# Masks of shifted attention windows as TensorE products, and layer 3's last addition on ScalarE, in a four-layer image kernel

## Chip, core and metric

The kernel runs on one core of one Trainium2 chip. The time is device microseconds from launch to end; the smaller the better. The median of the runs shown is 4648.1 us. All data are 32-bit floats.

The core has five engines that run side by side and wait for one another by semaphores: TensorE (PE: products, with its weight loads listed apart as PEld), VectorE (DVE), ScalarE (ACT), GpSimd (POOL), and SyncE (SP), whose queue issues the DMAs here. Products land in PSUM, of which the kernel uses six single banks and one pair of banks.

## What is computed

32 images of 56 x 56 pixels and 96 channels go through four layers. Cut to what matters here:

```python
# layer 0: mixture of 4 experts by a router; 96 -> 384 channels, 3x3 depthwise, 384 -> 96
rw = sigmoid(mean(x) @ Wr + br)
h = relu(bn(x @ (rw-mixed Wpw) + ...)); h = relu(bn(depthwise3x3(h, rw-mixed Wdw) + ...))
x = x + bn(h @ (rw-mixed Wpwl) + ...)
# layer 1: x + depthwise 5x5; layer 2: relu, depthwise 3x3, 96 -> 96 product, batch norm
# layer 3: one block of shifted-window attention
shifted = roll(x, (-3, -3)); win = 7x7 windows (64 of them, 49 pixels each)
h = layernorm(win); q, k, v = h @ wq, h @ wk, h @ wv          # 3 heads of 32
attn = softmax(q k^T / sqrt(32) + mask)     # mask: -inf between pixels of different groups
res = x + unroll((attn v) @ wo + bo)
x = res + gelu(layernorm(res) @ w1 + b1) @ w2 + b2
```

The mask matters only in windows of the last column (their pixels with column >= 4 come from the other side of the image) and of the last row (row >= 4 likewise); the corner window has four groups.

## The kernel before

Four stages run as a software pipeline over the images: the router of one image, the conditional layer 0 of the image before it, the depthwise layers 1 and 2 of the one before that, and layer 3 (called swin) of the oldest. Each stage is a Python generator that records its work; `interleave` gives each piece of work a target from `PLAN` (start and length of each stage, in images). The class `Recorder` then lays out one fixed order for each engine: it runs through a model of the engines with the costs of `COST`, takes at each moment the ready work with the lowest target, and uses `CROSSING` for the time from one engine's end to another's start and `TO_TENSOR` for that to TensorE. Nothing is decided on the chip: each engine works through its list, waiting by semaphore. As every recorded instruction is issued by `give`, all of them have one line in the profile, L578, and are told apart by tile names.

Two kinds of filler are written into the orders. If the model's TensorE has nothing to do for `SPARE_AFTER` ns, a spare product is put in (identity by identity, 128 x 128, rows banks<-ident). Between two long taps on VectorE other work, or else a one-element fill (breath), is put in. Both are then executed whether or not the chip needs them. A 32-bit product shows as two matmul records and two weight loads.

What works where, by names of tiles:

- Layer 0: matmuls banks<-xT,wmix (96 to 384 channels), ScalarE into h; nine taps of the depthwise filter on h, one on ScalarE and eight on VectorE (h<-h,mix,h, 1568 elements, 48 an image); matmuls banks<-h,wmix, added to xT by VectorE. All of xT is rearranged by DMA for layers 1 and 2.
- Layers 1 and 2: matmuls banks<-x,band in 32 x 32 sub-arrays, four banks at a time; ScalarE moves the outputs; DMAs into filtered; matmul banks<-pw,filtered into res. The weights pw have a 97th column, so that res carries, beside 96 values centred on their mean, the mean itself.
- Layer 3 by rows of windows, i = 0 to 7: `norm1` and `turn1` (ScalarE squares lnsq, VectorE sum var, GpSimd power and product lnd, TensorE transposes banks<-ident,lnd); products with wq, wk, wv; `exponentials`: scores banks<-qT,kT, 24 products (8 windows by 3 heads) in one group of sub-arrays of 32 rows by 64 columns, three banks, then ScalarE's exp into exps; `kept`: GpSimd multiplies exps by a mask of zeros and ones, in rows 0 to 6 only the last window (exps<-exps,keep_column), in row 7 all (keep_last); `averaged`: sums of exponentials (pair<-exps,ones) and weighted values (pair<-exps,v) into the one pair of banks, ScalarE's log and exp for the reciprocal; `divided`: three VectorE operations that end in oT and free the pair; `attended`: product with wo, added to res.
- The end of layer 3 in chunks of 4 and 3 tiles of 112 pixels, `hidden` and `perceptron`: products with w1, ScalarE's gelu into hid, products with w2 (banks<-w,hid). GpSimd writes tb = res + b2; VectorE then adds, for each of the 4 or 3 tiles, the bank, the mean (the 97th column of res) and tb; SyncE sends tb out. There are two tb buffers.

The constants of the order, and the lines at the end of layer 3 that the change touches:

```python
CROSSING = 136
TO_TENSOR = {"vector": 981, "gpsimd": 1497, "scalar": 453, "sync": 1437}
SPARE_AFTER = 318
...
tbs = ring("tb", [LT, 4, C], 2)
...
chip.gpsimd.tensor_tensor(tb, src[:, :, :C], b2[:LT, None, :].to_broadcast([LT, n, C]), ALU.add)
...
for j in range(n):
    chip.vector.scalar_tensor_tensor(
        tb[:, j], pt[:LT, j * C : (j + 1) * C], src[:, j, C:], tb[:, j], ALU.add, ALU.add
    )
```

Of the kernel before, what the change touches and what calls it, by code (L numbers as in the profile page):

```python
# [13 lines left out]
AF = mybir.ActivationFunctionType  # L14
ALU = mybir.AluOpType
# [4 lines left out]
C = 96  # L20
# [3 lines left out]
P = 128  # L24
NB = 3
NROW = 8
RT = 7 * W
PK = 98
NP = 4
LT = 2 * W  # L30
NL = 7
PW = 14
WT = 49
NWIN = 8
SLOT = 64
PS = SLOT + WT
# [9 lines left out]
NH = 3  # L46
HD = C // NH
# [3 lines left out]
NEG = -1e30  # L51
# [22 lines left out]
    return m  # L74


def window_keeps():


    r, c = np.divmod(np.arange(WT), 7)  # L80
    last = np.zeros((P, NP, WT), np.float32)
    column = np.zeros((P, WT), np.float32)
    for j in range(NP):
        for at in range(2):
            group = np.where(r >= 4, 2, 0) + np.where((c >= 4) & (j == NP - 1) & (at == 1), 1, 0)
            last[SLOT * at : SLOT * at + WT, j] = group[:, None] == group[None, :]
    column[SLOT : SLOT + WT] = (c[:, None] >= 4) == (c[None, :] >= 4)
    return last, column


def banded(k, back):
# [67 lines left out]
LANDING = 2200  # L159
IMAGE_LANDING = 10000  # L160

PLAN = {"router": (-0.309, 1.019), "conditional": (0.642, 1.103), "depthwise": (1.462, 1.483), "swin": (3.316, 0.933)}
CROSSING = 136

TO_TENSOR = {"vector": 981, "gpsimd": 1497, "scalar": 453, "sync": 1437}
SPARE_AFTER = 318
RUN = 1
CHANGE = 170
SAME = 0.0
BESIDE = {(32, 32): 16, (32, 64): 6, (64, 32): 6, (32, P): 3, (P, 32): 3, (P, P): 1}  # L170


# [409 lines left out]
def kernel(  # L582
# [10 lines left out]
    def ring(name, shape, n):  # L593
        return Ring([const.tile(shape, F32, name=f"{name}{k}") for k in range(n)])
# [15 lines left out]
    qTs = ring("qT", [C, RT], 2)  # L610
    kTs = ring("kT", [C, RT if general else NWIN * SLOT], 2)
    vs = ring("v", [P, NP, C], 3)
    tbs = ring("tb", [LT, 4, C], 2)
    x3s = ring("x3", [P, NQ, NBLK, W + 3], 2)
    oTs = ring("oT", [C + 1, 2 * RT], 2)
    x1s = ring("x1", [P, NQ, NBLK, W + 4], 2)
# [48 lines left out]
    for at, name in (  # L665
# [4 lines left out]
        src = a[name]  # L670
        if len(src.shape) == 1:
            src = src.rearrange("(o m) -> o m", o=1)
        elif len(src.shape) == 4:
            src = src.rearrange("e a b m -> (e a b) m")
        nc.sync.dma_start(out=rows[at : at + src.shape[0]], in_=src)
    c384 = const.tile([P, NB, NV], F32, name="c384")
    for k in range(NB):
        pt = mm.tiles[k]
# [4 lines left out]
    for at, name in (  # L683
# [4 lines left out]
        src = a[name]  # L688
        if len(src.shape) == 1:
            src = src.rearrange("(o m) -> o m", o=1)  # L690
        elif len(src.shape) == 4:
            src = src.rearrange("a b o m -> (a b o) m")
        nc.sync.dma_start(out=rows96[at : at + src.shape[0]], in_=src)
    c96 = const.tile([C, NU], F32, name="c96")
    pt = mm.tiles[3]
# [31 lines left out]
    pt = mm.tiles[5]  # L727
# [11 lines left out]
    def later(shape, src, name):  # L739
        return hold(const.tile(shape, F32, name=name), src)  # L740
# [14 lines left out]
    pt = mm.tiles[4]  # L755
# [15 lines left out]
    b2 = later([P, C], a["L3_conv_b2"].partition_broadcast(P), "L3_conv_b2")  # L771
    if general:
        masks = later([PK, 2, NP * PK], layouts["mask"].rearrange("l q j k -> q l (j k)"), "masks")
    else:
        keep_last = later([P, NP, WT], layouts["keep_last"], "keep_last")
        keep_column = later([P, WT], layouts["keep_column"], "keep_column")

        slots = ring("slots", [C, NWIN, SLOT], 3)

        exps = ring("exps", [P, NH, NP, WT], 2)  # L780
        ones32 = const.tile([P, HD], F32, name="ones32")
# [61 lines left out]
    chip = Recorder(nc)  # L843
# [326 lines left out]
    def stage_swin(b, res):  # L1170
# [52 lines left out]
        def exponentials(i):  # L1223

            qT, kT = rows_of[i][:2]
            pss = [chip.new(mm) for _ in range(NH)]
            with chip.together():
                for j in range(NP):
                    for at in range(2):
                        n = 2 * j + at  # L1230
                        for h in range(NH):
                            hs = slice(h * HD, (h + 1) * HD)
                            chip.tensor.matmul(
                                pss[h][SLOT * at : SLOT * (at + 1), j * WT : (j + 1) * WT],
                                kT[hs, SLOT * n : SLOT * (n + 1)],
                                qT[hs, WT * n : WT * (n + 1)],
                                start=True,
                                stop=True,
                            )
            e = exps_of[i] = chip.new(exps)  # L1240
            for h in range(NH):
                chip.scalar.activation(
                    e[:, h].rearrange("k j q -> k (j q)").part(h),
                    pss[h][:, : NP * WT],
                    AF.Exp,
                    scale=1.0 / math.sqrt(HD),
                    reads=(tables,),
                )

        every = tuple(range(NH))  # L1250

        def kept(i):
            e = exps_of[i].part(*every)
            if i < NROW - 1:
                ks = slice(SLOT, PS)
                view = e[ks, :, NP - 1]
                chip.gpsimd.tensor_tensor(
                    view, view, keep_column[ks, None, :].to_broadcast([WT, NH, WT]), ALU.mult
                )
                return  # L1260
            keep = keep_last.rearrange("k j q -> k (j q)")
            view = e.rearrange("k h j q -> k h (j q)")
            chip.gpsimd.tensor_tensor(view, view, keep[:, None, :].to_broadcast([P, NH, NP * WT]), ALU.mult)

        def averaged(i):

# [138 lines left out]
        def perceptron(i):  # L1405
            src, n = chunk(res, i)
            tb = chip.new(tbs)[:, :n]
            chip.gpsimd.tensor_tensor(tb, src[:, :, :C], b2[:LT, None, :].to_broadcast([LT, n, C]), ALU.add)
            active = [hiddens.pop((i, k)) for k in range(NB)]
            pt = chip.new(mm)  # L1410
            with chip.together():
                for j in range(n):
                    for k in range(NB):
                        chip.tensor.matmul(
                            pt[:LT, j * C : (j + 1) * C],
                            active[k][:, j * LT : (j + 1) * LT],
                            w2[:, k],
                            start=(k == 0),
                            stop=(k == NB - 1),
                        )  # L1420
            for j in range(n):
                chip.vector.scalar_tensor_tensor(
                    tb[:, j], pt[:LT, j * C : (j + 1) * C], src[:, j, C:], tb[:, j], ALU.add, ALU.add
                )
            to = out[b, i // 2].rearrange("(j p) c -> p j c", p=LT)
            chip.sync.dma_start(out=to[:, 4:] if i % 2 else to[:, :4], in_=tb)

# [2 lines left out]
        exps_of, turned_out = {}, {}  # L1430
# [58 lines left out]
        for i in range(NROW + 1) if general else ():  # L1489
            before, here, after = i > 0, i < NROW, i + 1 < NROW  # L1490
# [40 lines left out]
        for i in range(NROW + 2) if not general else ():  # L1531
            here, after = i < NROW, i + 1 < NROW
            if here:
                exponentials(i)
                yield 1.5
            if after:
                project_q(i + 1)
                yield 2
            if here:
                kept(i)  # L1540
            if i + 3 < NROW:
                norm1(i + 3)
                yield 1
            if after:
                project_v(i + 1)
                yield 1
            if 0 < i <= NROW:
                averaged(i - 1)
                yield 1.5
                divided(i - 1)  # L1550
                yield 1
            if i > 1:
                attended(i - 2)
                yield 1.5
            if i >= NROW - 1:
                norm2(i - NROW + 1)
                yield 1
            turn1(i + 2)
            yield 0.5
# [36 lines left out]
    def when(stage, b):  # L1596

        start, length = PLAN[stage]
        return b + start, length
# [23 lines left out]
def build(nc, shapes, batch):  # L1623

    a = {k: nc.dram_tensor(f"in_{k}", s, F32, kind="ExternalInput").ap() for k, s in shapes.items()}
    layouts = {
        k: nc.dram_tensor(f"in_{k}", s, F32, kind="ExternalInput").ap()
        for k, s in (
            ("mask", (2, PK, NP, PK)), ("keep_last", (P, NP, WT)), ("keep_column", (P, WT)),
            ("k5", (P, NSLOT, 5, 2 * BIN)), ("k3", (P, NSLOT, 3, 2 * BIN)), ("centre", (P, 2 * BIN)),  # L1630
        )
    }

    out = nc.dram_tensor("out", (batch, NROW // 2, 2 * RT, C), F32, kind="ExternalOutput").ap()
    with tile.TileContext(nc) as tc, tc.tile_pool(name="flags", bufs=1) as flags:
        in_range = flags.tile([1, 1], mybir.dt.int32, name="in_range")
        tile_scores_in_range(tc, a, in_range)
        kernel(tc, a, layouts, out, False)

        with tc.If(nc.values_load(in_range[:1, :1]) < 1):  # L1640
            kernel(tc, a, layouts, out, True)
# [23 lines left out]
```

## Time and profile before

| | |
|---|---|
| runs shown | 4643.1, 4648.1, 4649.3 us; median 4648.1 |
| profiled execution, its own time | 4639.0 us |
| its span, first to last instruction | 4637.2 us |
| mean granted TensorE clock | 0.992 |
| scores on TensorE (banks<-qT,kT) | 12288 records, 198.5 us busy |
| spare products (banks<-ident) | 1246 records, 170.7 us busy |
| masks on GpSimd | 224 of 1769 ns and 32 of 1508 ns on average |
| tb on GpSimd (res + b2) | 256, 1994 ns on average |
| tb on VectorE (bank + mean + tb) | 896, 308 ns on average |
| taps on VectorE | 1536, 1890 ns on average |

The span holds a start of some 0.3 ms in which the pipeline fills, a long steady part that repeats for each image, and an end in which only layers 1 to 3 are left. A share of busy time over the whole span mixes these. Where a row gives a count and a mean, their product can be more than the busy time, since matmuls of different sub-arrays overlap. In a row of waits the three numbers are the sum in us, how often, and the longest. In the busy time by window, each engine's us is followed by its instructions; the granted clock, the DMA share and GB/s come last. In the timeline, an item is start, duration, engine, line, operation, tiles, shape and count, and in brackets the idle time before it with what ended it.

### The profile page before, as it was taken

The page shows a single profiled execution, that of the slowest core. Times are in us where ns is not written, and L with a number is a line of the kernel's source. Part 1 is how long each engine was busy: PE and PEld are TensorE (multiplying, and loading weights), DVE is VectorE, ACT ScalarE, POOL GpSimd, SP SyncE. Part 2 cuts the span into 40 slices and gives each one's busy share as a digit, 9 for nine tenths or more (in the row PEclk, how much of TensorE's full clock was granted, in tenths as well). Part 3 has the DMA queues.
Part 4 walks back from the last instruction along what each step waited for, and adds up shares of the span by engine and source line. Part 5 has one row for each costly group of instructions (what it writes and reads, how often), then busy time and mean ns, then how long its engine had stood idle before and what let it go on. Part 6 is the DMA issues. An engine that isn't in the chain of part 4 may idle for free. (4 is left out here: it accounts for less than half of the span.)

```text
span 4637.2 us, 166483 instructions
## 1 busy us (share of the span) xinstructions
PE 4489.9 (97%) x71978; PEld 3168.6 (68%) x71978; DVE 4061.4 (88%) x5444; ACT 3393.6 (73%) x6625; POOL 2967.1 (64%) x1855
## 2 busy tenths in 40 slices
PE   5799999999999999999999999999999999999999
PEld 3566767676767676666676766666766676766677
DVE  6999999998999998999998999988999999999733
ACT  2467777777777777777787777777777787777666
POOL 3035767666767766767766767766767666767633
PEclk8999999999999999999999999999999999999999
DMA  2112111122111122211121211121211122211110
GB/s 54 34 39 45 41 43 32 39 48 45 44 41 30 38 47 45 45 40 30 38 47 45 46 40 30 38 45 45 46 41 30 38 45 45 46 41 31 28 36 22
DMA packets 556411, 185.36 MB, mean 40 GB/s; under 512 B 551679, under 2 KB 552340, under 8 KB 552596
## 3 DMA queue, kind: packets, MB, share of 16 engines
q1 hardware_dynamic: 555668, 174.61, 16.9%
q8 instruction: 569, 9.32, 0.9%
q14 instruction: 174, 1.43, 0.1%
HBM read 42.37 MB, written 38.54 MB: 17 GB/s over the span
## 5 line engine op out<-in xcount | busy, mean ns | idle before, releaser
L578 DVE SCALAR_TENSOR_TENSOR h<-h,mix,h 128x1568 f32<-128x1568 f32 x1536 | 2892.2, 1890 | 18.7 <-ACT h L578 13.0
L578 POOL TENSOR_TENSOR var<-var,mhalf 112x4 f32<-112x4 f32 (+1 forms) x512 | 1068.8, 2093 | 195.4 <-DVE var L578 182.8
L578 POOL TENSOR_TENSOR lnd<-res,var 112x384 f32<-112x384 f32 (+1 forms) x512 | 779.1, 1528 | 524.7 <-PE banks L578 503.0
L578 ACT ACTIVATE hid<-banks,c 128x448 f32<-128x448 f32 (+1 forms) x768 | 446.4, 589 | 346.5 <-PE banks L578 340.4
L578 PE MATMUL banks<-xT,wmix 96*128 96x392 f32 (+1 forms) x1536 | 644.2, 519 | 5.7 <-DVE wmix L578 4.5
L578 PE MATMUL banks<-hT,w 96*128 96x448 f32 (+1 forms) x1536 | 641.0, 507 | 3.7
L578 PE MATMUL banks<-x,band 32*32 32x280 f32 x24576 | 611.7, 408 | 14.8 <-issue 7.7
L578 PEld LDWEIGHTS banks<-w,hid 128*112 128x112 f32 x5376 | 563.9, 178 | 75.9 <-issue 46.2
L578 POOL TENSOR_TENSOR tb<-res,L_conv_b 112x384 f32<-112x384 f32 (+1 forms) x256 | 506.3, 1994 | 160.0 <-DMA out<-tb 139.1
L578 PE MATMUL banks<-w,hid 128*112 128x96 f32 x5376 | 576.2, 262 | 5.1 <-ACT hid L578 4.6
L578 PE MATMUL banks<-h,wmix 128*96 128x392 f32 x1536 | 548.4, 497 | 11.6 <-ACT h L578 11.6
L578 ACT ACTIVATE h<-banks,bias,s 128x392 f32<-128x392 f32 (+1 forms) x768 | 518.3, 690 | 39.0 <-PE banks L578 29.6
L578 PEld LDWEIGHTS banks<-x,band 32*32 32x32 f32 x24576 | 385.0, 103 | 226.7 <-issue 50.7
L578 POOL TENSOR_TENSOR exps<-exps,keep_column 49x147 f32<-49x147 f32 x224 | 396.2, 1769 | 204.1 <-ACT exps L578 194.0
L578 ACT ACTIVATE h<-h,biasd,s 128x784 f32<-128x784 f32 x384 | 389.3, 1038 | 114.0 <-DVE breath L578 83.6
L578 PEld LDWEIGHTS banks<-h,wmix 128*96 128x96 f32 x1536 | 246.5, 164 | 248.6 <-issue 207.2
L578 PEld LDWEIGHTS banks<-xT,wmix 96*128 96x128 f32 x1536 | 266.0, 192 | 134.0 <-issue 57.6
L578 DVE TENSOR_REDUCE var<-lnsq 112x4 f32<-112x388 f32 (+1 forms) x512 | 253.7, 496 | 113.3 <-ACT lnsq L578 59.8
L578 ACT ACTIVATE h<-h,mix 128x1568 f32<-128x1568 f32 x192 | 308.6, 1607 | 60.4 <-PE banks L578 46.4
L578 DVE SCALAR_TENSOR_TENSOR tb<-banks,res,tb 112x96 f32<-112x96 f32 x896 | 246.6, 308 | 109.2 <-PE banks L578 103.9
L578 PEld LDWEIGHTS banks<-hT,w 96*128 96x128 f32 x1536 | 252.5, 191 | 128.9 <-issue 69.1
L578 PEld LDWEIGHTS banks<-ident,lnd 112*96 112x96 f32 x1792 | 197.5, 126 | 157.0 <-issue 127.3
(135 smaller groups left out, 6653.0 us busy)
## 6 DMA issues: line engine op xcount, KB each, us to landing
x<-xT SPq DMA_DIRECT2D x1536, 35.0 KB
xT<-in_x SPq DMA_DIRECT2D x32, 1176.0 KB
filtered<-x SPq DMA_DIRECT2D x960, 35.0 KB
out<-tb SPq DMA_DIRECT2D x128, 168.0 KB
out<-tb SPq DMA_DIRECT2D x128, 126.0 KB
filtered<-x SPq DMA_DIRECT2D x576, 7.0 KB
band<-in_k SPq DMA_DIRECT2D x1, 960.0 KB
wpw<-in_L_conv_Wpw SPq DMA_DIRECT2D x1, 576.0 KB
```

The costliest lines, as they stand in the source:

```text
L578: getattr(getattr(self.nc, w.engine), method)(*args, **kw)
```

## The change

The masks are no longer applied after the exponential but added to the scores before it. For each window that has groups, each head gets one more product, 4 group indicators of the keys by 4 rows of 0 or -1e30 of the queries (in sub-arrays of 32 rows and 64 columns like the scores; unused rows are zero), which accumulates on the score. In rows 0 to 6 that is the last window (3 products), in row 7 all eight (24). GpSimd's products by masks (`kept`) go.

At the end of layer 3, ScalarE writes tb = res + mean, one activation for each tile of 112 pixels; GpSimd adds b2 to tb in place; VectorE adds the bank to all of tb in one instruction. There are three tb buffers in place of two.

The constants of the order (`PLAN`, `CROSSING`, `TO_TENSOR`, `SPARE_AFTER`) have other values, so that the lists of all engines are laid out anew. The title of the change also names layer 0's product in whole columns; no line of layer 0 differs.

```diff
-PLAN = {"router": (-0.309, 1.019), "conditional": (0.642, 1.103), "depthwise": (1.462, 1.483), "swin": (3.316, 0.933)}
-CROSSING = 136
-TO_TENSOR = {"vector": 981, "gpsimd": 1497, "scalar": 453, "sync": 1437}
-SPARE_AFTER = 318
+PLAN = {"router": (-0.16, 0.924), "conditional": (0.642, 1.103), "depthwise": (1.452, 1.424), "swin": (3.369, 1.066)}
+CROSSING = 412
+TO_TENSOR = {"vector": 926, "gpsimd": 798, "scalar": 129, "sync": 1437}
+SPARE_AFTER = 431
...
-def window_keeps():
+def window_groups():
...
+    keys = np.zeros((C, 4, SLOT), np.float32)
+    queries = np.zeros((C, 4, WT), np.float32)
+    for kind in range(4):
+        group = np.where(c >= 4, 1, 0) * (kind % 2) + np.where(r >= 4, 2, 0) * (kind // 2)
+        for h in range(NH):
+            for g in range(4):
+                keys[h * HD + g, kind, :WT] = group == g
+                queries[h * HD + g, kind] = np.where(group == g, 0.0, NEG)
+    return keys, queries
...
-    tbs = ring("tb", [LT, 4, C], 2)
+    tbs = ring("tb", [LT, 4, C], 3)
...
-        keep_last = later([P, NP, WT], layouts["keep_last"], "keep_last")
-        keep_column = later([P, WT], layouts["keep_column"], "keep_column")
+        group_keys = later([C, 4, SLOT], layouts["group_keys"], "group_keys")
+        group_queries = later([C, 4, WT], layouts["group_queries"], "group_queries")
...
                         n = 2 * j + at
+                        kind = int(n == NWIN - 1) + 2 * int(i == NROW - 1)
                         for h in range(NH):
...
+                            into = pss[h][SLOT * at : SLOT * (at + 1), j * WT : (j + 1) * WT]
                             chip.tensor.matmul(
-                                pss[h][SLOT * at : SLOT * (at + 1), j * WT : (j + 1) * WT],
+                                into,
                                 kT[hs, SLOT * n : SLOT * (n + 1)],
                                 qT[hs, WT * n : WT * (n + 1)],
                                 start=True,
-                                stop=True,
+                                stop=not kind,
+                            )
+                        for h in range(NH if kind else 0):
+                            hs = slice(h * HD, (h + 1) * HD)
+                            into = pss[h][SLOT * at : SLOT * (at + 1), j * WT : (j + 1) * WT]
+                            chip.tensor.matmul(
+                                into, group_keys[hs, kind], group_queries[hs, kind], start=False, stop=True
                             )
...
-        def kept(i):
-            e = exps_of[i].part(*every)
-            if i < NROW - 1:
-                ks = slice(SLOT, PS)
-                view = e[ks, :, NP - 1]
-                chip.gpsimd.tensor_tensor(
-                    view, view, keep_column[ks, None, :].to_broadcast([WT, NH, WT]), ALU.mult
-                )
-                return
-            keep = keep_last.rearrange("k j q -> k (j q)")
-            view = e.rearrange("k h j q -> k h (j q)")
-            chip.gpsimd.tensor_tensor(view, view, keep[:, None, :].to_broadcast([P, NH, NP * WT]), ALU.mult)
...
             tb = chip.new(tbs)[:, :n]
-            chip.gpsimd.tensor_tensor(tb, src[:, :, :C], b2[:LT, None, :].to_broadcast([LT, n, C]), ALU.add)
+            for j in range(n):
+                chip.scalar.activation(tb[:, j], src[:, j, :C], AF.Identity, bias=src[:, j, C:])
+            chip.gpsimd.tensor_tensor(tb, tb, b2[:LT, None, :].to_broadcast([LT, n, C]), ALU.add)
...
-            for j in range(n):
-                chip.vector.scalar_tensor_tensor(
-                    tb[:, j], pt[:LT, j * C : (j + 1) * C], src[:, j, C:], tb[:, j], ALU.add, ALU.add
-                )
+            chip.vector.tensor_tensor(
+                tb, pt[:LT, : n * C].rearrange("p (j c) -> p j c", c=C), tb, ALU.add
+            )
...
-            if here:
-                kept(i)
```

## The prediction

> **What bounds the kernel now.** I read the page's busy shares first, then one steady stretch of the busy times by window, the list of waits, and last the timeline of TensorE.
>
> ```profile
> span 4637.2 us, 166483 instructions
> PE 4489.9 (97%) x71978; PEld 3168.6 (68%) x71978; DVE 4061.4 (88%) x5444; ACT 3393.6 (73%) x6625; POOL 2967.1 (64%) x1855
> ...
> 2000.00:2500.00 500.00, 494.33 (x8254) 347.30 (x8253) 457.73 (x595) 381.45 (x751) 346.65 (x205) 1.00 0.19 42
> ...
> PE pair L578 <- DVE oT L578: 24.8, 35, 2.4
> ACT hid L578 <- PE banks L578: 340.4, 258, 2.6
> POOL lnd L578 <- PE banks L578: 503.0, 110, 7.7
> DVE tb L578 <- PE banks L578: 103.9, 58, 4.8
> ```
>
> The window row is one of five like it: TensorE 494 of 500 us, VectorE 458, ScalarE 381, GpSimd 347, granted clock 1.00. The waits say who waits for whom: ScalarE, GpSimd and VectorE all wait mostly for TensorE's banks, while TensorE waits little for anyone. A busy matmul row is a modelled end, so I checked with starts:
>
> ```profile
> 2000.24 0.77 PE L578 MATMUL banks<-qT,kT 32*64 32x49 f32 x48
> 2000.94 0.59 PE L578 MATMUL banks<-ident,lnd 112*96 112x112 f32 x4
> ...
> 2005.37 1.29 PE L578 MATMUL banks<-ident 128*128 128x128 f32 x10
> 2006.49 0.92 PE L578 MATMUL banks<-xT,wmix 96*128 96x448 f32 x2
> ...
> 2158.53 1.29 PE L578 MATMUL banks<-ident 128*128 128x128 f32 x10
> 2160.41 0.55 PE L578 MATMUL pair<-exps,ones 49*32 49x196 f32 x12 [0.59 <-DVE oT L578]
> ```
>
> Each group starts where the one before it ends its stream, so TensorE's order is a chain of fixed lengths with few holes. The steady period is 138.8 us an image (the keep_last product of image 10 starts at 1766 us, that of image 20 at 3154). The rows also price what the change touches on TensorE. A score group of 24 products (48 records) holds it 0.70 us, 29 ns a product. Five spare products (10 records) hold it 1.12 us, 224 ns each. A second run of five is followed by a true wait of 0.59 us for oT, that is for the one pair buffer, once an image.
>
> So the question is what the changed order adds to and takes from TensorE's chain; the other engines matter only where they make it wait.
>
> **The change, part by part.** Counts come from the program's orders, which are fixed before it runs.
>
> 1. Mask products on TensorE. Rows 0 to 6 of an image get 3 more products, row 7 gets 24: 45 an image, 1440 in all, in the chain itself. At the group's mean (29 ns) row 7 costs 24 x 29 = 0.70 us. But in the trace the first six rounds of a group start 58 ns apart for 6 records, and the last records 16 ns apart, as if the queue ran dry; added records come at the end, so 2 x 16.5 = 33 ns a product: 0.10 us for 3, 0.79 us for 24, 7 x 0.10 + 0.79 = 1.49 us an image, 48 us in all. Low bound: all at the fast rate, 2 x 9.75 ns, 28 us. High bound: a mask product follows the score product of the same sub-array, so each round of three takes what a round of six took; 3.0 us an image, 96 us. I take 48, by the nearest row.
>
> The Trainium skill speaks against this part: "TensorE: Matmul & The Clock Gate", Part 1, on the floor per matmul, gives about 25 ns from start to start however few columns. By it 2880 records would cost 72 us, and the sum below would be 24 us worse. The row has 48 records in 0.70 us, 14.6 ns each, across six sub-arrays, so here the row contradicts the floor and decides.
>
> 2. Fewer spares. The order holds 437 where it held 623. Outside the first two and last two of 33 equal parts of it they fall by some 120: 120 x 224 ns = 27 us off. The other 65 stand where TensorE waits anyway (it is busy 82.7 of the first 150 us), so I take 0 for them, 15 us at most.
>
> 3. Fewer switches of tiling, 1306 for 1367. A product of 392 columns is followed after 0.33 us by one of its kind and after 0.42 by a tiled one: 61 x 0.094 = 6 us off.
>
> 4. The wait for oT. In the changed order no spares stand before the sums of exponentials; other products fill that distance. From one such group to the next the chain takes 6.8 us in the trace (2021.71 to 2028.51); the tightest places of the new order hold some 6.0 us of TensorE work, and fewer of the chains have two of VectorE's long taps in them. I take 0.4 of the 0.59 us back, 32 x 0.4 = 13 us; bounds 19 off and 26 added (0.8 us an image, if the tight place waits in full).
>
> 5. GpSimd loses 224 products of 1.77 us and 32 of 1.51 us, 444 us. The list of TensorE's waits has no masked exps in it, so they were covered by the groups between scores and sums, and I count nothing for them. Their relief to VectorE is small: its 1536 taps have a median of 1842 ns and a mean of 1890, so all that GpSimd's 1855 instructions disturb there is about 1536 x 48 ns = 74 us, hidden behind TensorE besides.
>
> 6. Layer 3's end. VectorE loses 896 x 308 ns = 247 us (1.23 us for a chunk of four) and gets 256 sums; the rows res<-banks,res of like size, 552 and 454 ns, make that 128 x 1.00 = 128 us. So it carries 119 us less, and a bank of the last product is free 0.68 us sooner. ScalarE gets 896 activations; its row lnsq<-res from SBUF is 523 ns for 384 columns and 445 for 288, hence some 290 for 96 (390 at most, by the 56-column row with scale and bias): 260 us, 8.1 us an image, 73% to 79% busy. They start from res, ready long before, into a third tb buffer; the cover is ScalarE's own idle time. GpSimd's sum keeps its size and loses its 139 us of waits for the output's DMA to the third buffer; they would go to ScalarE, which now writes tb first, if three were too few. The output DMAs are as many. Two loads of 98 and 75 KB replace 98 and 25 KB at the start, behind others.
>
> What do earlier banks and a lighter VectorE give TensorE? Its small holes that I can see by comparing equal groups come to about 3 us an image, half of it at the two filters, which need four of the six banks. I take 0.6 us an image off, 20 us in all; bounds 0 and 40.
>
> Sum against the profiled execution: 4637.2 + 48 - 27 - 6 - 13 - 20 = 4619 us of span. The median of the runs shown, 4648.1, stands 10.9 above that span (1.8 of it around the span in the same run, the rest from run to run). So 4630.
>
> **The rivals.** A measurement of this kernel tells about 0.2%, 9 us, from no change.
>
> A. *It cancels.* The added products are paid back by the spares and nothing more is gained: 48 - 27 - 6 - 13 = +2, so 4648, and 4640 to 4657 as its range. For it: parts 1 to 4 are all that is countable. Against: banks are released earlier. That the diff lacks the "whole columns" of layer 0 named in its title belongs here: layer 0's product is the same in both, worth nothing.
>
> B. *ScalarE at layer 3's end makes TensorE wait* (slower). Place: the stretch of w1 and w2 products, where gelu outputs are ScalarE's.
>
> ```profile
> 2000.00:2017.05 17.05, 17.00 (x339) 12.31 (x337) 16.93 (x20) 15.48 (x31) 12.81 (x8) 1.00 0.13 27
> ...
> 2102.30:2119.35 17.05, 17.05 (x99) 12.19 (x98) 13.22 (x28) 10.11 (x16) 10.86 (x9) 1.00 0.14 33
> 2119.35:2136.40 17.05, 17.05 (x252) 10.22 (x250) 16.39 (x28) 14.79 (x31) 11.63 (x7) 1.00 0.04 9
> ```
>
> ScalarE is busy 15.5, 10.1 and 14.8 of 17.05 us there, so 10.8 us are free for 8.1 more: enough on average, not everywhere. If a quarter is exposed, 2 us an image, 65 us: 4695. It decides from 0.9 us an image, where the 18 us of the forecast and the 9 us of noise are used up. Against it: ScalarE waits 340 us in all for those banks, so it is ahead of TensorE.
>
> C. *The masks cost their high bound* (slower): +48, and the oT wait stays, +13: 4691.
>
> D. *VectorE was the pacer.* 91% busy in the window, and 119 us plus 132 dropped one-element fills of 59 ns, 8 us, come off: 4648 - 127 = 4521. Against: its own list of waits is headed by TensorE.
>
> The Trainium skill would favour D: "Perfetto Trace Analysis", Identifying the Most-Contended Engine, holds matmul occupancy to be a poor measure of headroom and weight-load busy time, 68% on this page, a good one. By it TensorE has room, the masks and spares would be worth nothing, and the sum would be D's. The starts above leave no such room, and the trace decides.
>
> **How the numbers follow.** Forecast 0.45, A 0.16, B 0.19, C 0.13, D 0.07. Faster by over 0.2% is the forecast and D, 0.52; within, A, 0.16; slower, B and C, 0.32. The forecast's own range is 4569 (masks at 28, all the wait gone, 15 us in the ramps, 20 more from holes: 61 less) to 4638. The range reaches to B and C: 4570 to 4700; D and a ScalarE exposed by more than that are left out.
>
> **What would show it.** TensorE still busy some 494 of 500 us; the score groups with masks 0.1 us longer in seven rows and 0.8 in one; 874 records of spares; no 0.59 us before the sums of exponentials; VectorE near 3940 us, ScalarE near 3650, GpSimd near 2520; tb no longer waiting for its DMA. The prediction is wrong if TensorE's idle time grows with ScalarE's hid or kT as releaser (B), if groups with masks take twice as long (C), or if TensorE's work per image falls by more than its products explain (D).

## The result, and the profile after

| | before | after |
|---|---|---|
| median (lowest to highest) | 4648.7 us (4643.1 to 4653.6) | 4858.4 us (4826.8 to 4861.3) |
| ratio, 95% interval | | 1.0434 (1.0398 to 1.0470) |
| one image in the steady part | 138.8 us | 145.3 us |
| mean granted clock | 0.992 | 0.978 |

The change costs 210 us. The prediction, 4630 us with 4700 as its upper end, was wrong in sign. First the page of the changed kernel: its span, and the busy time of each engine.

```profile
span 4824.8 us, 171166 instructions
...
PE 4548.9 (94%) x74486; PEld 3200.2 (66%) x74486; DVE 3932.3 (82%) x4672; ACT 3584.0 (74%) x7521; POOL 2237.2 (46%) x1599
```

The span is 187.6 us longer; the profiled execution was the fastest of the changed kernel, 4826.8 us. TensorE is 59.0 us busier, so it is idle 128.6 us more. VectorE has lost 129 us and GpSimd 730 us, and neither shortened the time. Two stretches of the changed kernel, in the busy time by window:

```profile
2000.00:2500.00 500.00, 476.29 (x7489) 332.10 (x7489) 406.96 (x472) 377.04 (x788) 247.34 (x170) 0.96 0.17 38
2500.00:3000.00 500.00, 483.63 (x8027) 339.35 (x8026) 431.33 (x504) 390.12 (x823) 241.66 (x167) 1.00 0.17 38
```

TensorE's 494 of 500 us have become 476 and 484, and the clock is 0.96 in the first. What TensorE waits for between 1000 and 4000 us, before:

```profile
PE pair L578 <- DVE oT L578: 12.9, 22, 0.6
PE banks L578 <- issue: 6.5, 14, 0.9
PE banks L578 <- ACT hid L578: 3.8, 23, 0.2
PE pair L578 <- issue: 3.1, 7, 0.8
```

and in the same stretch of the changed kernel:

```profile
PE banks L579 <- issue: 36.5, 41, 4.7
PE banks L579 <- ACT hid L579: 32.4, 42, 1.2
PE banks L579 <- ACT slots L579: 22.6, 21, 1.1
PE pair L579 <- issue: 17.3, 23, 1.4
```

The wait for oT is gone. Two new kinds stand in its place: 55 us in which ScalarE is late (hid and slots), and 54 us of "issue", in which the trace shows nothing that TensorE waits for, with holes up to 4.7 us. The experiments follow these two.

### The profile page after: what moved, and what is told of

Read it like the earlier page. It is cut to its first block, busy times and chain, and to the rows that moved or that the text cites. A ratio compares the mean times of both kernels' runs of the same rounds, so it can differ in the third digit from the quotient of the medians.

```text
span 4824.8 us, 171166 instructions
## 1 busy us (share of the span) xinstructions
PE 4548.9 (94%) x74486; PEld 3200.2 (66%) x74486; DVE 3932.3 (82%) x4672; ACT 3584.0 (74%) x7521; POOL 2237.2 (46%) x1599
## 4 chain that ended last, share of the span: by engine, by line
PE 66%; ACT 17%; issue 7%; DVE 4%; SPq 2%; DMA 2%; POOL 1%; ACTq 0%; POOLq 0%; DVEq 0%
PE banks L579 63%; ACT h L579 6%; PE pair L579 3%; DVE h L579 3%; ACT hid L579 3%; SPq L579 2%; ACT xT L579 2%; DMA filtered<-x 1%; ACT slots L579 1%; ACT exps L579 1%; ACT v L579 1%; ACT L579 1%; ACT kT L579 1%; ACT qT L579 0%; ACT x L579 0%
## 5 line engine op out<-in xcount | busy, mean ns | idle before, releaser
L579 POOL TENSOR_TENSOR var<-var,mhalf 112x4 f32<-112x4 f32 (+1 forms) x512 | 987.2, 1934 | 728.7 <-DVE var L579 657.3
L579 POOL TENSOR_TENSOR lnd<-res,var 112x384 f32<-112x384 f32 (+1 forms) x512 | 599.5, 1173 | 678.7 <-PE banks L579 648.9
L579 POOL TENSOR_TENSOR tb<-tb,L_conv_b 112x384 f32<-112x384 f32 (+1 forms) x256 | 509.2, 1998 | 706.7 <-ACT tb L579 706.7
L579 PE MATMUL banks<-x,band 32*32 32x280 f32 x24576 | 638.5, 422 | 43.6 <-issue 41.8
L579 PE MATMUL banks<-hT,w 96*128 96x448 f32 (+1 forms) x1536 | 641.5, 505 | 26.8 <-ACT hid L579 26.8
L579 ACT ACTIVATE hid<-banks,c 128x448 f32<-128x448 f32 (+1 forms) x768 | 456.2, 595 | 150.6 <-PE banks L579 146.2
L579 PEld LDWEIGHTS banks<-xT,wmix 96*128 96x128 f32 x1536 | 275.9, 196 | 235.7 <-issue 106.1
L579 DVE TENSOR_TENSOR hid<-pair,hid 96x392 f32<-96x392 f32 x256 | 143.1, 559 | 221.4 <-ACT hid L579 219.8
L579 ACT ACTIVATE x<-banks 128x280 f32<-128x280 f32 x384 | 130.4, 415 | 248.3 <-PE banks L579 248.3
L579 ACT ACTIVATE lnsq<-res 112x384 f32<-112x384 f32 (+1 forms) x512 | 250.1, 491 | 71.5 <-DVE var L579 67.3
```

The costliest lines, as they stand in the source:

```text
L579: getattr(getattr(self.nc, w.engine), method)(*args, **kw)
```

## The experiments

All ratios are to the kernel before, measured together with each run (medians 4645.8 to 4654.8 us). "Holes" is TensorE's idle time in stretches of over 150 ns, between 1000 and 4000 us of the trace's own time, which begins some 11 us before the span; the lists of waits go by the span. (In the changed kernel a hole of 4.8 us lies between the two starts; by the span its holes are 112.0 us, 55.6 of them at an edge.) "At an edge" is the part of it that ends just where a block of 256 of TensorE's instructions has been read; how that is found stands under *Load and instructions*. "Clock lost" is (1 - mean clock) x span, an estimate of the time that it costs.

| run | median us | ratio (95%) | holes us | at an edge | clock lost us |
|---|---|---|---|---|---|
| before | 4648.7 | | 26.8 | 10.1 | 37 |
| after | 4858.4 | 1.0434 (1.0398 to 1.0470) | 116.8 | 60.4 | 106 |
| e1_consts_only | 5033.0 | 1.0827 (1.0806 to 1.0849) | 155.1 | 67.1 | |
| e2_old_consts | 4774.1 | 1.0273 (1.0253 to 1.0293) | 67.2 | 30.9 | |
| e3_masks_only | 4715.6 | 1.0140 (1.0117 to 1.0163) | 60.4 | 4.0 | |
| e4_tb_only | 4761.7 | 1.0247 (1.0226 to 1.0268) | 56.8 | 12.0 | |
| e5_masks_in_place | 4695.1 | 1.0102 (1.0078 to 1.0125) | 30.2 | 13.8 | 42 |
| e6_tb_in_place | 4729.3 | 1.0165 (1.0131 to 1.0199) | 59.4 | 12.6 | 61 |
| e7_both_in_place | 4782.0 | 1.0293 (1.0256 to 1.0330) | 55.8 | 10.3 | 72 |
| e8_new_plan_only | 4907.1 | 1.0554 (1.0523 to 1.0585) | 172.8 | 86.6 | |
| e9_old_plan | 4700.4 | 1.0105 (1.0080 to 1.0130) | 47.5 | 10.1 | |
| e10_before_new_plan | 4953.9 | 1.0663 (1.0635 to 1.0691) | 157.3 | 93.7 | 128 |
| e11_before_new_times | 4712.0 | 1.0132 (1.0113 to 1.0152) | 49.5 | 15.7 | |
| e12_no_spares | 4758.5 | 1.0234 (1.0210 to 1.0258) | 55.0 | 7.5 | 176 |
| e13_load_later | 4987.5 | 1.0733 (1.0704 to 1.0762) | 209.4 | 32.5 | |
| e14_load_later_new_plan | 5049.4 | 1.0861 (1.0831 to 1.0891) | 203.0 | 35.4 | |
| e15_depthwise_target | 5106.0 | 1.0983 (1.0955 to 1.1012) | 197.7 | 4.0 | |
| e16_swin_target | 4918.9 | 1.0586 (1.0543 to 1.0629) | 123.2 | 69.4 | |
| e17_load_in_pieces | 4769.2 | 1.0261 (1.0242 to 1.0280) | 99.3 | 44.1 | 57 |
| e18_pieces_new_plan | 4836.6 | 1.0403 (1.0379 to 1.0428) | 111.0 | 42.8 | 87 |

### Constants or code

The first question was whether the two parts cost, or the order laid out anew. The kernel before with all constants of the change, and the changed code with those of before:

```diff
-PLAN = {"router": (-0.309, 1.019), ..., "depthwise": (1.462, 1.483), "swin": (3.316, 0.933)}
-CROSSING = 136
+PLAN = {"router": (-0.16, 0.924), ..., "depthwise": (1.452, 1.424), "swin": (3.369, 1.066)}
+CROSSING = 412
...
```

> The code of before with the four changed constants of the order (PLAN, CROSSING, TO_TENSOR, SPARE_AFTER); masks and tb as before. Theory O (the order): the constants alone bring the new waits of TensorE, so this is slower than before by 2% or more, 4740 to 4870 us, with TensorE near 480 of 500 us in a steady window and holes of 5 us or more an image. Theory S (ScalarE's 896 more activations) and theory M (the mask products): the constants are harmless without the new code, 4600 to 4680 us.

> The changed code (masks by TensorE, tb by ScalarE, three tb buffers) laid out with the constants of before. Theory O: back near before, 4600 to 4700 us, TensorE 490 of 500 us or more in a steady window. Theory S and theory M: still slow, 4780 us or more, since the added work is all there. If both O and S hold in part, some 4720 to 4780 us.

Then one part of the code each, with before's constants: the masks without the end of layer 3, and the end of layer 3 without the masks.

> Before with its own constants and only the masks moved to TensorE; tb as before. Theory M: the slow-down is here, 4780 us or more. Theories O and S: 4620 to 4690 us; the mask products' 118 ns for three and some 0.8 us for 24, with 12 spares fewer in all, are worth about 50 us at most and GpSimd's shorter path gives some back.

> Before with its own constants and only the end of layer 3 changed: res plus mean by ScalarE, one sum by VectorE, three tb buffers; masks by GpSimd as before. Theory S: the slow-down is here, 4780 us or more, with TensorE waiting for ScalarE's hid and kT. Theories O and M: 4600 to 4680 us; 896 x 377 ns = 338 us more on ScalarE is covered by its 27% of idle time.

The constants alone cost the old code 384 us; the changed code with the old constants still costs 125 us, the masks alone 67, the end of layer 3 alone 113. Both parts lose and the constants lose, but every one of these runs has an order of its own, which hides what the edit itself does.

### The parts inside the order of before

So the next runs keep before's order of every engine, instruction by instruction, and swap only what is written at the places concerned. For the masks, in the group of scores and at GpSimd's place:

```diff
+            swap = chip.work[-1].swap = []
...
+                            swap.append(("tensor", "matmul", (into, *pair), {"start": not mask, ...}))
...
+                chip.work[-1].swap = []    # keep_column, keep_last
```

For tb, three buffers in turn:

```diff
+            for j in range(n):
+                swap.append(("scalar", "activation", (tb[:, j], src[:, j, :C], AF.Identity), {"bias": src[:, j, C:]}))
+            swap.append(("gpsimd", "tensor_tensor", (tb, tb, b2[:LT, None, :].to_broadcast([LT, n, C]), ALU.add), {}))
...
+            chip.work[-n].swap.append(
+                ("vector", "tensor_tensor", (tb, pt[:LT, : n * C].rearrange(...), tb, ALU.add), {})
```

> Before with every list of every engine in before's own order, spares included; the mask products are put into the score groups where they stand and GpSimd's mask products are left out where they stood. Nothing is laid out anew. Theory W (the work itself): the products lengthen TensorE's chain by 48 us and nothing hides it, 4680 to 4715 us, as the masks alone cost with a new order (67 us). Theory L (the new layout did it): 4640 to 4670 us.

> Before's own order again; where GpSimd wrote tb, ScalarE's activations and GpSimd's sum in place stand, where VectorE began its 4 or 3 additions stands its one sum, and tb takes three buffers in turn. Theory W: ScalarE's 338 us more make TensorE wait wherever they stand, 4720 us or more, as the tb part alone cost with a new order (113 us). Theory L: 4630 to 4670 us, since ScalarE has 27% idle and VectorE's bank is free earlier.

> Both parts of the change in before's own order: all of the changed kernel's work, none of its layout. Theory W: near the changed code with before's constants, 4750 us or more. Theory L: 4650 to 4720 us, the sum of the two parts alone, so that 140 us or more of the changed kernel's 210 are its layout.

The masks in place cost 48.0 us (4695.1 - 4647.1). One group of scores in that run's timeline of TensorE:

```profile
2013.67 0.77 PE L594 MATMUL banks<-qT,kT 32*64 32x49 f32 x48
2014.24 0.33 PE L594 MATMUL banks<-group_queries,group_keys 32*64 32x49 f32 x6
```

The group ends 0.13 us after its scores would. The same run's busy time from 2000 to 2500 us:

```profile
2000.00:2500.00 500.00, 494.90 (x8294) 349.19 (x8293) 451.28 (x600) 380.74 (x750) 277.49 (x171) 1.00 0.17 38
```

TensorE is as full as before (494.9 of 500 us), so nothing hides the added products, while the 69 us that GpSimd lost in this window (347 to 277) show nowhere.

The tb part in place costs 82 us (4729.3 - 4647.1). In its groups of instructions, ScalarE's new ones (busy time, mean of one, idle before):

```profile
L581 ACT ACTIVATE tb<-res 112x96 f32<-112x96 f32 x896 | 263.0, 373 | 0.0
```

One takes 373 ns, but their rows overlap, and together they hold the engine 263 us. ScalarE is never idle before one: their input has long been there. What stands behind them waits. ScalarE and TensorE, from two timelines of this run, merged here by start:

```profile
2129.05 1.17 ACT L581 ACTIVATE tb<-res 112x96 f32<-112x96 f32 x4
...
2131.32 0.76 PE L581 MATMUL banks<-hT,w 96*128 96x336 f32 x2
...
2133.16 0.91 ACT L581 ACTIVATE tb<-res 112x96 f32<-112x96 f32 x3
2133.62 0.54 PE L581 MATMUL banks<-w,hid 128*112 128x96 f32 x4
2133.95 0.68 ACT L581 ACTIVATE h<-banks,bias,s 128x392 f32<-128x392 f32 x1
2134.52 0.53 ACT L581 ACTIVATE lnsq<-res 112x384 f32<-112x384 f32 x1
2134.93 0.54 ACT L581 ACTIVATE hid<-banks,c 128x336 f32<-128x336 f32 x1
2135.52 1.62 PE L581 MATMUL banks<-w,hid 128*112 128x96 f32 x14 [1.36 <-ACT hid L581]
```

The w1 product of 336 columns (banks<-hT,w) ends at 2132.08, and its gelu (hid, 336 columns) could start there. It starts at 2134.93, behind three tb activations and other work of ScalarE's queue, and TensorE stands 1.36 us until it ends. The same products in the kernel before, where ScalarE's queue holds the same but for tb:

```profile
2088.35 0.76 PE L578 MATMUL banks<-hT,w 96*128 96x336 f32 x2
...
2090.00 0.54 PE L578 MATMUL banks<-w,hid 128*112 128x96 f32 x4
2090.70 1.61 PE L578 MATMUL banks<-w,hid 128*112 128x96 f32 x14 [0.16 <-ACT hid L578]
```

There the gelu starts 1.75 us after its product, at 2090.10; with tb it is 3.61 us, and the wait of 0.16 us has become 1.36. Instruction by instruction, the four tb activations at 2129.05 put ScalarE off by 1.06 us and the three at 2133.16 by 0.80. The list of TensorE's waits in this run, 1000 to 4000 us:

```profile
PE banks L581 <- ACT hid L581: 34.7, 44, 1.4
PE banks L581 <- ACT kT L581: 12.1, 21, 0.6
```

3.8 us have become 46.8. This is the prediction's rival B, place and mechanism, with nothing but the tb part changed in the order.

Both in place cost 135 us, the sum of 48 and 82 and 5 more. So 76 of the 210 us come with the new layout (4858.4 - 4782.0).

### Which constants

The changed code with PLAN alone new, and with all new but PLAN; the code of before with PLAN alone new, and with CROSSING, TO_TENSOR and SPARE_AFTER new:

> The changed code with before's CROSSING, TO_TENSOR and SPARE_AFTER; of the constants only PLAN is the changed one. If the times to TensorE are what hurts (they tell the layout that ScalarE's outputs reach TensorE after 129 ns instead of 453): back at 4774 us, as with all constants of before. If PLAN hurts: 4840 to 4860 us, as the changed kernel.

> The changed code with before's PLAN; CROSSING, TO_TENSOR and SPARE_AFTER as changed. With e8 (4907 us) this splits the constants. Theory P (the stages' targets hurt): 4740 to 4800 us, as with all constants of before (4774). Theory T (the times to TensorE hurt): 4830 us or more. Theory F (the constants fit only together, any mixture is worse than either set): above 4858.

> The code of before with the changed PLAN alone. Theory P: most of the 386 us that all changed constants cost that code, 4900 us or more, with holes of TensorE at the filters (x,band) of 3 us an image or more. Theory T: under 4720 us.

> The code of before with the changed CROSSING, TO_TENSOR and SPARE_AFTER and its own PLAN. Theory P: 4640 to 4740 us. Theory T: 4900 us or more.

PLAN is what costs: 158 us in the changed code (4858.4 - 4700.4), 299 in that of before. The other three cost the old code 57 us, but in the changed code they bring 74 (4774.1 to 4700.4). The best that the change reached is thus e9, still 46 us slower than before. It is also faster than both parts in before's order (e7): TensorE's waits for hid between 1000 and 4000 us are 9.5 us in e9 and 33.5 in e7. So the price of the tb part depends on where the layout puts it. What e9 has instead is 22.9 us of waits for oT. Two runs asked which stage of PLAN it is, in the changed code with the other new constants:

```diff
-PLAN = {..., "depthwise": (1.452, 1.424), "swin": (3.369, 1.066)}
+PLAN = {..., "depthwise": (1.452, 1.424), "swin": (3.316, 0.933)}    # e15, router of before
+PLAN = {..., "depthwise": (1.462, 1.483), "swin": (3.369, 1.066)}    # e16, router of before
```

> The changed code and times with before's PLAN except the depthwise stage's target. With before's whole PLAN it took 4700, with the changed one 4858. If the filters' earlier and denser place does it: 4800 us or more. If the router's later target (its load) or swin's does it: 4680 to 4740.

> The same with only swin's target changed (later start, longer). If it does it: 4800 us or more; if the filters or the router do: 4680 to 4740.

Each is worse alone than all three together. The stages' targets depend on one another, so no stage can be named; the router's alone wasn't tried. Nor do all bad orders fail in the same way: e15 has 197.7 us of holes and only 4.0 at an edge.

### Load and instructions

What is the "issue" in which TensorE waits for nothing? One such hole in the changed kernel's timeline of TensorE:

```profile
2000.12 0.72 PE L579 MATMUL banks<-x,band 32*32 32x280 f32 x23
2004.51 3.50 PE L579 MATMUL banks<-x,band 32*32 32x280 f32 x73 [3.68 <-issue]
```

TensorE stops after 23 of 96 records of one filter group. SyncE's queue in the same timeline, just before:

```profile
1995.96 0.34 SPq L579 DMA_DIRECT2D xT<-in_x  x1
```

That is the load of the next image, 1.2 MB. The same time by windows of 6 us; the last three numbers are clock, DMA share and GB/s:

```profile
1991.00:1997.00 6.00, 6.00 (x231) 3.70 (x205) 5.59 (x5) 1.28 (x4) 2.56 (x3) 0.90 0.30 63
1997.00:2003.00 6.00, 3.84 (x128) 2.48 (x128) 2.65 (x5) 4.59 (x9) 0.00 (x0) 0.95 0.89 204
2003.00:2009.00 6.00, 4.49 (x75) 2.48 (x75) 5.09 (x5) 0.00 (x0) 2.55 (x1) 0.50 0.06 13
```

The load fills the DMA engines (0.89), TensorE starves towards its end, and afterwards the clock is at 0.50. The page has one queue whose records fit TensorE:

```profile
q8 instruction: 588, 9.63, 0.8%
```

588 reads, each of 16,384 B in the trace. TensorE's records, weight loads and products and its few others, are 150,182 in this trace; 150,182 / 256 = 586.6. Before it is 569 reads and 145,142 / 256 = 567.0; the masks in place add 5760 records by the program (22.5 blocks; the trace has 5832 more) and 22 reads. So queue 8 brings TensorE's instructions, 256 to a read. The reads around the hole, from the trace's DMA records, with the number of TensorE's records started by then:

```
read   start     end       TensorE records before its start
229    1994.30   1995.59   58878
230    2001.83   2003.21   59329
231    2005.68   2006.62   59397
```

451 records were executed between two reads that bring 256. Counting records started less 256 for each read finished gives how far TensorE has eaten into what it holds. At the beginning of each of the five holes of over 2.5 us in this stretch of the changed kernel the count is 449, exactly the same each time; the next read ends, the count falls by 256 to 193, and TensorE resumes 1.2 to 1.5 us after it. All 17 holes of e10 of 2.45 us or more show 449 and 193 or 194 too. TensorE has run out of instructions. In the table a hole is at an edge when TensorE resumes at this place in a block. In none of the three traces does the count go beyond 449. In the kernel before it is 446 at the worst, and there is no such hole.

The load holds the reads up in all three kernels: in 59 of their 61 loads between 1000 and 4000 us no read begins from 1.5 to 5.5 us after the load's issue. What differs is how much TensorE takes meanwhile. In the kernel before:

```profile
2071.00:2077.00 6.00, 6.00 (x128) 4.31 (x125) 6.00 (x6) 4.90 (x9) 4.57 (x3) 1.00 0.93 213
```

The DMA engines are as full (0.93), but TensorE takes only some 250 records in 6 us, 277 between the reads at 2069.12 and 2077.25, so the late read isn't missed. One filter group lies under each load there too. But in the first 4 us after the issue TensorE takes 134 records on average (63 to 219), in the changed kernel 261 (200 to 319) and in e10 300 (199 to 347). The new PLAN lays more dense groups under the load.

Two pairs of runs tested the load. The first issued it five DMA issues later, just ahead of its first reader:

```diff
+                if w.landing == IMAGE_LANDING and w.calls:
+                    late, behind = [w], 0
+                    continue
...
+                if late and (behind > 8 or used):
+                    self.nc.sync.dma_start(out=kw["out"].found(), in_=kw["in_"])
```

> The changed kernel; each image load (xT<-in_x, 1.2 MB, the DMA engines 96% busy while it runs) is issued five DMA issues later, just ahead of its first reader. Theory I (while the load fills the DMA engines, TensorE's own instructions come late, and the dense filter groups run dry, which then halves the clock): the holes of 3.8 to 4.9 us inside x,band groups go, 4800 to 4840 us. Theory B (those holes are waits for banks or x): they stay, 4845 us or more, more still if the later load delays the router.

> The code of before with the changed PLAN alone (4954 us, a hole of 3 to 4.6 us inside an x,band group in nearly every image), with the image load five DMA issues later. Theory I: most of these holes go, 4 us and more an image with what they do to the clock: 4780 to 4870 us. Theory B: within 30 us of 4954.

Both are slower than without it, by 129 and 95 us, and tell little of the load itself. The edges did shrink (60.4 to 32.5 us, 93.7 to 35.4, none over 1.8 us), but ScalarE now stands 5.7 to 7.9 us in each image ahead of the load's first reader, and TensorE waits for what is queued there. (The trace names the load as releaser in 2 of these 20 waits, and in 18 a DMA into filtered, which this work doesn't read.) From the waits of e13:

```profile
PE banks L589 <- ACT hid L589: 154.3, 20, 9.2
```

The second pair left the load in place and cut each into eight DMAs, so that its rows are 1568 B and not 12,544 B:

```diff
+                    cols = [slice(n * HALF * W // 4, (n + 1) * HALF * W // 4) for n in range(8)]
+                    calls = [("dma_start", (), {"out": kw["out"][:, s], "in_": kw["in_"][:, s]}) for s in cols]
```

> The changed kernel with each image load issued as eight DMAs of 392 columns, one after the other where the one stood, so that a row of a packet is an eighth as long. Theory I (TensorE's instructions are read late behind the load's long packets): the four holes of 3.8 to 4.9 us inside x,band groups in 1000 to 4000 us shrink under 2 us, 4800 to 4850 us. Theory B (the load's traffic as such, or a bank, makes the hole): the same holes, within 20 us of 4858.

> The code of before with the changed PLAN alone, and the load in the same eight pieces. Theory I: the holes of 3 to 4.6 us inside x,band groups, one in nearly every image, shrink under 2 us and the granted clock rises, 4800 to 4900 us for 4954. Theory B: within 30 us of 4954.

The changed kernel gains 89 us (4858.4 to 4769.2), the kernel before with the new PLAN 117 (4953.9 to 4836.6). The filter group of e18 that stood 4.48 us in e10:

```profile
1431.38 2.22 PE L583 MATMUL banks<-x,band 32*32 32x280 f32 x93
1434.93 1.61 PE L583 MATMUL banks<-x,band 32*32 32x280 f32 x67 [1.32 <-issue]
```

and in e10:

```profile
1438.87 2.78 PE L578 MATMUL banks<-x,band 32*32 32x280 f32 x111
1446.13 2.40 PE L578 MATMUL banks<-x,band 32*32 32x280 f32 x49 [4.48 <-issue]
```

Edges of about 1.3 us remain, no hole at an edge is over 1.7 us, and the clock lost falls from 106 to 57 us and from 128 to 87. In all 41 loads of the two runs a read now begins from 1.5 to 5.5 us after the first issue. So the load was what held the reads up. Whether its long rows did it isn't separated: eight DMAs also take longer to issue (4.46 us in one load), which spreads the load. Nor is it the whole of the edges: the five long holes are 21 of the changed kernel's 60.4 us, the others are short. The Trainium skill ("Runtime: NRT & Kernel Launch", Instruction fetch mechanics) has the reads of 256 instructions by a DMA queue of the sequencer's own, and calls their cost mostly hidden. The size agrees with the count above. That they are hidden holds for most reads here, but 67 of 374 in 3000 us end a hole, 60.4 us in all.

### Spares

Before's order with the spares after the 310th of 623 left out; their products are used by nothing.

```diff
+                if w.engine == "tensor" and w.calls[0][1][1] is self.spare[0]:
+                    spares += 1
+                    if spares > 310:
+                        continue
```

> Before in its own order without the spare products after the 310th of 623, so without the ten of each image in the steady part; nothing else is touched and no output changes. By the sum of the prediction (224 ns each, but five of the ten stand where TensorE then waits for oT anyway): 1.1 us an image, 30 to 40 us off, 4605 to 4625 us. If all ten cost TensorE time: 65 us off, 4580 us. If TensorE waits at both places: no change. If the holes of up to 1.9 us lowered the granted clock: slower than before.

It is 104 us slower (4758.5 against 4654.8). The clock loses 139 us more than before; if all of that is lost time, the absent work itself brought about 35. The timeline of TensorE at one of its holes, one in each image:

```profile
1635.38 0.45 PE L583 MATMUL banks<-ident,lnd 112*96 112x112 f32 x3
1637.71 0.57 PE L583 MATMUL pair<-exps,ones 49*32 49x196 f32 x12 [1.87 <-DVE oT L583]
```

The busy time before and after the end of that hole, with the granted clock third from the end:

```profile
1630.00:1637.00 7.00, 5.75 (x135) 4.21 (x132) 6.97 (x9) 6.91 (x15) 2.55 (x3) 1.00 0.01 2
1638.00:1648.00 10.00, 10.00 (x130) 6.96 (x119) 7.85 (x9) 5.51 (x10) 7.61 (x6) 0.51 0.01 2
```

1.87 us of waiting for oT, where spares had stood; then ten us at half clock with TensorE fully busy. All 27 holes of this length between 300 and 4450 us are followed, within 4 us of their start, by 6.8 or 10.2 us at half clock: 259 us in that stretch, where the kernel before has 6.8.

## Why the prediction was wrong, by its own steps

1. *Masks, +48.* Right: 48.0 us in before's order (36 to 58 by the interval, so that it fits to the us is luck). The extra 0.13 us of a group is near the 0.10 of the working, and the floor of 25 ns for a record, 72 us in all, is refuted. Rival C falls.
2. *Fewer spares, -27.* The count was right, 874 records. The price lacked a term: a spare also keeps the clock up. e12's 313 absent spares brought about 35 us and cost 139 by the clock, by the estimate above. The changed kernel's own clock loss is another matter: of its 121 us at half clock after the first 300 us, 109 begin in a hole at an edge or up to 2.4 us after one, and none after a wait for oT. So no loss is seen there that comes from its 186 absent spares.
3. *Switches, -6.* Too small to be seen in any of these runs.
4. *The wait for oT, -13.* The wait went entirely (12.9 us to none), but TensorE's waits put down to "issue" ahead of the same pair of banks rose from 3.1 to 17.3 us. Nothing was gained.
5. *GpSimd's masks, nothing.* Right: e5 shows it with VectorE and ScalarE untouched.
6. *Layer 3's end.* Sizes right: VectorE is at 3932 us against 3940 expected, ScalarE's activations hold it 263 us in e6 against 260, the third buffer ended the waits for the output's DMA. (896 x 308 ns is 276 us; the 247 of the working is the row's busy time, 246.6.) The conclusion was wrong, and this is the step that failed first: "the cover is ScalarE's own idle time". The idle time is there, but not where the new work stands; in a queue kept in order the gelu waits behind work that nobody needs yet. Instead of 20 us gained by earlier banks, 82 us were lost. Rival B had the place, and its 65 us the size within 17; it got 0.19 since ScalarE's 340 us of waits for banks were taken as a lead, a mean over the image. In e6 264 us of those waits are still there over the whole span, beside the 47 that TensorE loses to ScalarE between 1000 and 4000 us.
7. *What had no term.* Beyond its counts of parts 2 to 4 the sum took the new constants as neutral. In the changed code PLAN alone costs 158 us and all of them together 84 (4858.4 against 4774.1). The orders are fixed before the kernel runs, so that what TensorE executes while the image load runs can be read from them; the prediction didn't set the two beside each other.

Of the signs named beforehand, ScalarE at 3584 us (3650 expected) and GpSimd at 2237 (2520) came lower still, and TensorE's 494 of 500 failed; that ScalarE's hid appears as releaser was the sign given for B. Rival D falls: VectorE is 129 us lighter and the time longer. The page of the Trainium skill that favoured it ("Perfetto Trace Analysis", Identifying the Most-Contended Engine) misleads here: by it TensorE had room, with weight loads at 68% of the span, yet the small products of the masks cost 48 us. Rival A's sum of +2 gives 4650 and not 4648, which changes nothing.

The account of the 210 us is an estimate, with the sums of 1000 to 4000 us scaled to 32 images (by 1.55 after, 1.48 before): ScalarE's lateness 55.0 against 3.8 us, +80; edges of instruction blocks 60.4 against 10.1, +79; oT -19; clock +69; masks +48; spares and switches -33. That is 224, some of it counted twice, since parts of the holes lie in the time at half clock. The scaled numbers are also high: counted from 300 us on, TensorE's waits for ScalarE are 74 us against 8 and the edges 85 against 12. And all of it rests on the profiled executions, which lie 188 us apart. For the new layout alone the same account, after against both parts in before's order, gives +78 for edges (60.4 against 10.3 us), +16 for ScalarE (55.0 against 45.6), +34 for the clock and -33 for spares and switches: 95, counted twice in part likewise, where the medians are 76 us apart and the profiled executions 58. By this account the edges are the largest part of the layout's price; their exact share stays open.

What stays open: why the targets of the stages fit only together; whether the load's long rows or its issue in one piece held up the reads; and whether the kernel before would gain from a load in pieces, which wasn't tried. No version run here beats the kernel before.

## What to carry to other kernels

An engine's idle time is cover only if it lies just where the new work stands: look up what is queued behind the new instructions and who waits for it. If a change also lays an order out anew, the layout is a part of the change with a price of its own; write the edit into the old order to measure it by itself. Where TensorE runs dense groups of small products, see what the DMA engines carry at that moment: here its instructions were read by the same engines, and one load of 1.2 MB held the reads up until it starved.

## What the hardware showed beyond that

- In the changed kernel and in e10, each hole of over 2.5 us for want of instructions began at the same count, 449 records started beyond the blocks read to the end; TensorE resumed 1.2 to 1.5 us after the read ended. In 59 of 61 loads of an image in one DMA, no such read began from 1.5 to 5.5 us after the load's issue.
- The granted clock fell to half for 6.8 or 10.2 us after each of 27 holes of 1.87 us of waiting (e12). The Trainium skill ("TensorE: Matmul & The Clock Gate", Why this matters for your kernels) asks for no gaps of over some 3 us to avoid that; e12 has 259 us at half clock between 300 and 4450 us without one such hole.
- ScalarE's activation of 112 x 96 elements from SBUF with a bias takes 373 ns in its row, but 896 of them hold the engine 263 us, 294 ns each.
